# Direct transfers moved from GpSimd's queue to SyncE's and ScalarE's in a perceiver block with routed experts

## The chip, the cores and the metric

The kernel runs on one core of a Trainium2 chip. The metric is the time on the device in microseconds, of which the median of several runs is given. Three engines and the DMA queues matter here beside TensorE (PE): VectorE (DVE), ScalarE (ACT) and GpSimd (POOL) compute, and each of ScalarE, GpSimd and SyncE (SP) can also issue DMA transfers from its own queue of instructions, in the order in which they stand there.

## What is computed

All arrays are fp32. `x` has 8 batches of 64 rows of 512; `ctx_1024` has 8 batches of 1601 rows. The reference, cut to its three steps:

```python
x = x + xattn(layernorm(x), ctx_1024)   # 16 heads of 32; "stablemax" in place of softmax
x = x + attn(layernorm(x))              # 8 query heads of 64, one k and one v, causal softmax
x = x + ffn(layernorm(x))               # 2 shared experts (mean) + top 2 of 8 routed experts

# stablemax: s = where(x >= 0, x + 1, 1 / (1 - x));  s / sum(s)
# ffn:
shared = mean over 2 of gelu(xf @ sW1 + sb1) @ sW2 + sb2      # 512 -> 2048 -> 512
gates = xf @ rW + rb; the two largest, softmax of the two
moe = sum over the two of prob * (gelu(xf @ W1[e] + b1[e]) @ W2[e] + b2[e])
```

## The kernel before

The 512 rows of `x` stand in SBUF as `res`, four tiles of 128. The kernel has three stages.

**Attention.** The context is taken in 24 sections of 512 columns (three for each batch), each loaded as `cx` (L147) by SyncE. Keys and values of a section are made by `products` (L337): a product of two by two blocks in seven units, for which GpSimd makes differences of the context, `tx` (`context_part`, L313), and VectorE those of the weights. Scores of a section go through `convert` (L525): ScalarE splits them in sign, VectorE takes the reciprocal (L538), GpSimd adds (L539) and keeps the totals (L551). The first section is done plainly (`first_keys`, `first_values`), and between its units stand the norms of the four tiles (`first_rows`, L473: factors `ln_rs`, rows `xn`, transposed rows `xnT`) and the queries (`q_unit`, L484, the product `ps_q`). Each batch has 65 columns more than its three sections: 64 come in pairs of batches as `cxt` (`load_tail`, L421), and the last one of each batch, the odd column, is gathered at the start for all batches as `odd_x` (L415, four transfers of elements that lie apart in memory). Its value row is made once (`odd_v`) and copied by a transfer into the last row of the tail's values `vt` (L461). `clear` (L234), in the plan at the fourth batch, writes zeroes into the slots `xs` (4 MB in DRAM) and into one row each of `ys_d` and `yo_d`.

**Order.** A `Plan` holds the units of TensorE with a length each, and other steps with a due time; it calls them in that order. This is the order of the code's calls only: when the program is built, the framework places each instruction on its engine's queue by its own view of when it is ready, and allots buffers and waits. A queue is then run in that order, and an instruction that waits holds all behind it on its engine.

**Routing.** After the last norm the gates choose two experts for each row. VectorE works out a slot for each pair (`route`, L982), and GpSimd scatters the rows `xn` into `xs` with eight indirect transfers (L1069). The experts stand in the order of how many rows they have and get 256, 192, 160, 144 and four times 128 slots.

**Experts.** `run` (L1313) goes over the blocks: a shared expert on the last 128 rows (`Shared`), one half of the second shared expert (`Halves`), eight routed blocks (`Routed`), and the other half (`Halves`). A routed block takes 16 chunks of its hidden width; for each, TensorE makes `ps_h` (L1340), ScalarE takes the Gelu into `hT` (L1345), and TensorE adds the second product one chunk later (`second`). Weights come in quarters of 1 MB from SyncE (`w1t`, `w2t`, L775 and L783). Three steps move rows: `start` (L1259) fetches a block's rows `xg` from `xs` and transposes them, three chunks ahead of the block; `answer` (L1273) copies a result from PSUM to `yo` and writes it to `ys_d`; `turn` (L1304) first transposes results of blocks whose size is no multiple of 128, and is kept in the list `later` until chunk 3 of the block that follows. At the end `combine` (L1367) gathers the answers `g` from `ys_d` with eight indirect transfers and adds them to `res`, and `rows_out` stores it.

`xg`, `yo`, `g` and other tiles of 128 x 512 share five buffers (`sd`). All direct transfers of this account that are not named as SyncE's or ScalarE's are issued by GpSimd: biases and small weights at the start, `odd_x`, the zeroes, the rows into `vt`, `xg` and the answers. ScalarE issues only `wk`, `wv` and `wq` at the start.

Of the kernel before, what the change touches and what calls it, by code (L numbers as in the profile page):

```python
# [18 lines left out]
P = 128  # L19
# [9 lines left out]
NEXP, NSH = 8, 2  # L29
# [10 lines left out]
TAIL = SKV - NSEC * SEC  # L40
# [6 lines left out]
TOT = sum(CAPS)  # L47
# [28 lines left out]
def perceiver_kernel(  # L76
# [7 lines left out]
    nc = tc.nc  # L84
# [25 lines left out]
    def at4(name):  # L110
        return atp.tile([P, 1024], F32, tag="at", name=name)

    def np2(name):
        return npp.tile([P, 512], F32, tag="np", name=name)

    def sd(name):
        return sdp.tile([P, 512], F32, tag="sd", name=name)

    def psa(name):
        return ps_a.tile([P, 512], F32, tag="a", name=name)  # L120
# [35 lines left out]

    def bias_cols(src, n, name):
        t = const.tile([P, n], F32, name=name)
        nc.gpsimd.dma_start(out=t, in_=src)
        return t  # L160

    def bias_row(src, n, name):
        t = const.tile([P, n], F32, name=name)
        nc.gpsimd.dma_start(out=t, in_=src.partition_broadcast(P))
        return t

    bk_t = bias_cols(bk, NC, "bk_t")
    wv = load_w(wvT, "wv", nc.scalar)

    res = big.tile([P, NTT, E], F32, name="res")  # L170
    for tt in range(NTT):
        nc.sync.dma_start(out=res[:, tt, :], in_=x[tt * P : (tt + 1) * P, :])
    wq = load_w(wqT, "wq", nc.scalar)
    bq_t = bias_cols(bq, NC, "bq_t")
    bv_t = bias_cols(bv, NC, "bv_t")
    bo_t = sd("bo_t")
    nc.gpsimd.dma_start(out=bo_t, in_=bo.partition_broadcast(P))
    rb_t = bias_row(rb, NEXP, "rb_t")

    def load_small(src, name):  # L180
        t = const.tile([P, NC, src.shape[1]], F32, name=name)
        nc.gpsimd.dma_start(out=t, in_=src.rearrange("(c p) f -> p c f", p=P))
        return t

    rw_t = load_small(rW, "rw_t")
    b1_t = const.tile([P, NSH, NHC], F32, name="b1_t")
    nc.gpsimd.dma_start(out=b1_t, in_=sb1)

    ident = const.tile([P, P], F32, name="ident")
    make_identity(nc, ident)  # L190
# [11 lines left out]
    for j in range(2):  # L202
        m = mask[j * SQ : (j + 1) * SQ, 0, :]
        nc.gpsimd.affine_select(
            out=m, in_=m, compare_op=ALU.is_ge, fill=NEG, base=0,
# [10 lines left out]
        out=tri, in_=ones, compare_op=ALU.is_gt, fill=0.0, base=0,  # L216
# [12 lines left out]
    ys_d = dram.tile([TOT + 1, E], F32, name="ys_d")  # L229
    yo_d = dram.tile([P + 1, E], F32, name="yo_d")  # L230
# [3 lines left out]
    def clear():  # L234
        zero = np2("zero")
        nc.gpsimd.memset(zero, 0.0)
        nc.gpsimd.dma_start(
            out=xs.rearrange("(n p) e -> p n e", p=P),
            in_=zero.rearrange("p (o e) -> p o e", o=1).to_broadcast([P, ROWS // P, E]),
        )  # L240
        nc.gpsimd.dma_start(out=ys_d[TOT : TOT + 1, :], in_=zero[0:1, :])
        nc.gpsimd.dma_start(out=yo_d[P : P + 1, :], in_=zero[0:1, :])

    class Norm:

# [31 lines left out]
    def cols(t):  # L277
        return t.rearrange("p (c t) -> p c t", c=NC)
# [27 lines left out]
    def right_parts(x):  # L306
        return {"b11": x[:, 0:2, 0:HF], "b12": x[:, 0:2, HF:SEC],
                "b21": x[:, 2:4, 0:HF], "b22": x[:, 2:4, HF:SEC]}
# [101 lines left out]
    ROUND = TAIL - 1  # L410
# [1 line left out]

    odd_x = const.tile([P, NC, B], F32, name="odd_x")
    for c in range(NC):
        nc.gpsimd.dma_start(  # L415
            out=odd_x[:, c, :],
            in_=ctxT[:, c * P : (c + 1) * P, SKV - 1 : SKV].rearrange("b p s -> p (b s)"),
        )
    odd_v = const.tile([B, E], F32, name="odd_v")
# [31 lines left out]
    def tail_values(b):  # L451
        x = tails[b, "x"]
        ps = psa("ps_vt")
        for c in range(NC):
            nc.tensor.matmul(
                ps, x[:, c, 0 : 2 * ROUND], wv[:, c, :], start=c == 0, stop=c == NC - 1
            )
        for k in range(2):
            v = tails[b + k, "v"] = tlp.tile([P, E], F32, name="vt")
            nc.scalar.copy(v[:ROUND], ps[k * ROUND : (k + 1) * ROUND])  # L460
            nc.gpsimd.dma_start(out=v[ROUND:TAIL, :], in_=odd_v[b + k : b + k + 1, :])  # L461

    per = NSEC * SEC // P + 1

# [426 lines left out]
    for u, time in enumerate(when):  # L891
        plan.at(weighed[u], lambda u=u: weigh(*units[u]))
        plan.at(time, lambda u=u: begin(u))
        for j in range(1, 4):
            plan.at(time + 0.3 * j * wide[u] * step, lambda u=u, j=j: convert(*units[u], j))
        if u == 3 * nu:
            plan.at(time, clear)
    for tt in range(NTT):
        gap = 5.0 if tt < NTT - 1 else 3.2
        for bb in range(2):  # L900
            b = 2 * tt + bb
            last = (b + 1) * nu - 1
            done = weighed[last]
# [35 lines left out]
    from_i = gp.tile([P, 2, NTT], I32, name="from_i")  # L939
# [155 lines left out]
    class Shared:  # L1095
# [13 lines left out]
        def start(self):  # L1109
            self.x = xnT[:, :, self.tts[0] * P : self.tts[0] * P + self.n]  # L1110
# [21 lines left out]
    class Halves:  # L1132
# [55 lines left out]
        def combine(self):  # L1188

            k = len(self.right)  # L1190
            for q in self.qs:
                p = self.right[q] = right_parts(self.h[q])
                t = at4("ht").rearrange("p (k c s) -> p k c s", k=2, c=2)
                if not k:
                    self.t4 = at4("ht").rearrange("p (k c s) -> p k c s", k=2, c=2)
                p |= {"t1": t[:, 0], "t2": t[:, 1], "t3": p["b12"], "t4": self.t4[:, k]}
                k += 1
                for d, a, b in RIGHT:
                    nc.vector.tensor_tensor(p[d], p[a], p[b], ALU.subtract)
# [33 lines left out]
    class Routed:  # L1233
# [25 lines left out]
        def start(self):  # L1259
            self.x = at4("xgT").rearrange("p (c n) -> p c n", c=NC)  # L1260
            for s, w in self.parts:
                xg = sd("xg")
                nc.gpsimd.dma_start(out=xg[:w], in_=self.source(s, w))
                pt = cols(psx("pt_x"))
                for c in range(NC):
                    nc.tensor.transpose(pt[:, c, :w], xg[:w, c * P : (c + 1) * P], ident[:w, :w])  # L1266
                nc.vector.tensor_copy(self.x[:, :, s : s + w], pt[:, :, :w])  # L1267
            self.x = self.x[:, :, : self.n]
# [4 lines left out]
        def answer(self, s, w, src):  # L1273
            yo = sd("yo")
            nc.vector.tensor_copy(yo[:w], src)  # L1275
            nc.gpsimd.dma_start(out=self.dst[self.o0 + s : self.o0 + s + w, :], in_=yo[:w])  # L1276

        def second(self, hc, hT):
            first, last = hc == 0, hc == NHC - 1
# [28 lines left out]
                    nc.tensor.transpose(pt[:w, d, :], self.yT[:, d, s : s + w], ident)  # L1308
                self.answer(s, w, pt[:w].rearrange("p c d -> p (c d)"))

    later = []

    def run(blocks, at=None):  # L1313
        pending = None
        for n, blk in enumerate(blocks):
            if isinstance(blk, Halves):
                if n == 0:
                    blk.start()
                units = blk.units()
                for k, fn in enumerate(units):  # L1320
                    fn()
                    if pending is not None:
                        pending[0].second(*pending[1:])
                        pending = None
                    if at and (n, k) in at:
                        at[n, k]()
                    if k == 3:
                        while later:
                            later.pop(0)()
                    if k == len(units) - 3 and n + 1 < len(blocks):  # L1330
                        blocks[n + 1].start()
                continue
            for k, hc in enumerate(blk.hcs):
                w1t = blk.weights(hc // QC)[0]
                if k == 0 and n == 0:
                    blk.start()
                f = (hc % QC) * P
                ph = psa("ps_h")
                for c in range(NC):
                    nc.tensor.matmul(  # L1340
                        ph[:, : blk.n], w1t[:, c, f : f + P], blk.x[:, c, :],
                        start=c == 0, stop=c == NC - 1,
                    )
                hT = np2("hT")
                nc.scalar.activation(hT[:, : blk.n], ph[:, : blk.n], AF.Gelu, bias=blk.bias(hc))  # L1345
                if pending is not None:
                    pending[0].second(*pending[1:])
                pending = (blk, hc, hT)
                if at and (n, k) in at:
                    at[n, k]()  # L1350
                if k == 3:
                    while later:
                        later.pop(0)()
                if k == len(blk.hcs) - 3 and n + 1 < len(blocks):
                    blocks[n + 1].start()
        if pending is not None:
            pending[0].second(*pending[1:])
        while later:
            later.pop(0)()

    def expert_in(t, k):
        return lambda: nc.values_load(
# [19 lines left out]
    def routing():  # L1382
        for tt in range(NTT - 1):
# [10 lines left out]
            (0, 0): routing,  # L1394
            (2, 2): lambda: probabilities(tops.pop()),
            (2, 6): add_biases,
            (NEXP + 2, 1): lambda: combine(ys_d, from_i),
        },
    )

# [79 lines left out]
```

## Time and profile before

| | |
|---|---|
| time, median of 3 runs | 1409.54 us (1407.6 to 1409.95) |
| time of the profiled execution | 1412.35 us |
| its span | 1410.7 us |
| q1 (SyncE's queue) | 77732 packets, 136.94 MB |
| q0 (GpSimd's queue) | 4704 packets, 13.91 MB |
| q10 (ScalarE's queue) | 1632 packets, 3.15 MB |

Times of transfers, as the page gives them (median from issue to landing): `xs<-zero` 13.9 us, `xg<-xs` of 256 KB 6.9 us, `ys_d<-yo` of 256 KB 6.7 us, `odd_x` 7.9 us, `vt<-odd_v` 2.9 us, `w1t` of the routed experts 12.4 us, `wq` 15.0 us.

How to read the lines: times are microseconds unless a column is marked ns. A line of the timeline has start, length, engine, line of the code, operation, what it writes and reads, how many, and in brackets how long the engine was idle before it and what ended that. SPq and ACTq are the transfers that these engines issue; a transfer's length there is the time of its issue, not until it lands. A line of the waits has who waited for whom, the total, how many times and the longest. The chain is followed back from the last instruction, at each step to what released it; "issue" in it is time in which the engine waited for nothing that the profile shows. Numbers of buffers are left out of the names.

### The profile page before, as it was taken

How to read it: one execution, taken by the hardware profiler on the slowest of the kernel's cores; microseconds unless marked ns; L12 is line 12 of the kernel's file. 1: busy time of each engine (PE TensorE's matmuls, PEld its weight loads, DVE VectorE, ACT ScalarE, POOL GpSimd, SP SyncE). 2: the span in 40 equal slices, each digit the busy share in tenths (PEclk: the TensorE clock that was granted, in tenths of full speed). 3: DMA queues.
4: the chain of work that ended last, by engine and by line, in shares of the span. 5: the costliest groups of instructions: out<-in, count | busy, mean ns of one | idle time of the engine just before them, and what ended most of it. 6: DMA issues, size and time to landing. Idle time of an engine off the chain costs nothing.

```text
span 1410.7 us, 35571 instructions
## 1 busy us (share of the span) xinstructions
PE 1375.2 (97%) x15632; PEld 1084.2 (77%) x15632; DVE 887.1 (63%) x650; ACT 648.7 (46%) x1348; POOL 746.6 (53%) x672
## 2 busy tenths in 40 slices
PE   8999999999999999999999999999999999999996
PEld 3678788788788888788878877555786799977775
DVE  4698999898889997989988889514330000100331
ACT  3556566565666666765756567322211111122230
POOL 6388899885879886879886867400200000000020
PEclk9999999999999999999999999999999999999998
DMA  7002012102320121121121125353556256789620
GB/s 225 31 3 69 32 32 77 62 32 69 121 69 32 55 84 39 32 69 33 46 91 32 62 69 194 104 186 99 194 196 228 101 180 243 279 317 330 217 68 31
DMA packets 84226, 156.30 MB, mean 111 GB/s; under 512 B 13307, under 2 KB 13339, under 8 KB 84069
## 3 DMA queue, kind: packets, MB, share of 16 engines
q1 hardware_dynamic: 77732, 136.94, 28.5%
q0 software_dynamic: 4704, 13.91, 2.9%
q10 hardware_dynamic: 1632, 3.15, 0.7%
q8 instruction: 124, 2.03, 0.6%
q14 instruction: 34, 0.27, 0.1%
HBM read 143.24 MB, written 10.72 MB: 109 GB/s over the span
## 4 chain that ended last, share of the span: by engine, by line
PE 80%; issue 8%; DVE 4%; ACT 3%; POOL 3%; DMA 1%; POOLq 0%; DVEq 0%
PE ps_k L331 17%; PE ps_v L331 16%; PE ps_h L1340 8%; PE ps_s L520 5%; PE y L1294 4%; PE ps_hr L331 3%; PE ps_o L570 3%; PE ps_h L806 3%; PE y L1285 3%; PE y L818 3%; DVE neg L538 2%; PE ps_hh L331 2%; PE ps_v L399 1%; PE ps_k L389 1%; POOL tx L320 1%
## 5 line engine op out<-in xcount | busy, mean ns | idle before, releaser
L538 DVE RECIPROCAL neg<-neg 128x512 f32<-128x512 f32 (+1 forms) x224 | 684.0, 3092 | 65.5 <-ACT neg L537 57.4
L539 POOL TENSOR_TENSOR at<-at,neg 128x512 f32<-128x512 f32 (+1 forms) x224 | 266.6, 1195 | 136.8 <-DVE neg L538 129.4
L551 POOL TENSOR_TENSOR tot<-tot,at 128x512 f32<-128x512 f32 (+1 forms) x176 | 223.7, 1271 | 12.9
L1340 PEld LDWEIGHTS ps_h<-xgT,w1t 128*128 128x128 f32 x1024 | 147.8, 191 | 38.5 <-issue 33.2
L1345 ACT ACTIVATE hT<-ps_h,b1e 128x128 f32<-128x128 f32 (+4 forms) x128 | 50.3, 393 | 261.0 <-PE ps_h L1340 235.0
L537 ACT ACTIVATE neg<-neg,one_t 128x512 f32<-128x512 f32 (+1 forms) x224 | 161.3, 721 | 0.0
L1340 PE MATMUL ps_h<-xgT,w1t 128*128 128x128 f32 (+4 forms) x1024 | 160.7, 300 | 0.0
L535 ACT ACTIVATE neg<-ps_s 128x512 f32<-128x512 f32 (+1 forms) x224 | 129.5, 579 | 64.5 <-PE ps_s L520 53.8
L1276 POOL DMA_DIRECT2D ys_d<-yo x12 | 6.6, 546 | 287.2 <-DVE yo L1275 287.2
L331 PE MATMUL ps_k<-tx,sk 128*128 128x256 f32 x552 | 129.2, 385 | 5.7 <-ACT kT L348 5.7
L536 ACT ACTIVATE at<-ps_s 128x512 f32<-128x512 f32 (+1 forms) x224 | 130.9, 586 | 0.1
L331 PE MATMUL ps_v<-sv,tx 128*128 128x256 f32 x552 | 128.8, 384 | 0.0
L331 PEld LDWEIGHTS ps_k<-tx,sk 128*128 128x128 f32 x552 | 101.7, 190 | 24.8 <-ACT kT L348 3.8
L331 PEld LDWEIGHTS ps_v<-sv,tx 128*128 128x128 f32 x552 | 102.6, 190 | 16.5 <-issue 1.9
L1285 PE MATMUL y<-w2t,hT 128*128 128x512 f32 x192 | 96.5, 597 | 0.0
L1267 DVE COPY xgT<-pt_x 128x512 f32<-128x512 f32 (+3 forms) x12 | 6.8, 593 | 142.7 <-PE pt_x L1266 142.7
L348 ACT ACTIVATE kT<-ps_k,bk_t 128x256 f32<-128x256 f32 x138 | 59.4, 496 | 69.1 <-PE ps_k L331 69.1
L344 ACT COPY v<-ps_v 128x512 f32<-128x512 f32 x92 | 55.6, 604 | 70.2 <-PE ps_v L331 70.2
L331 PE MATMUL ps_k<-cx,wk 128*128 128x256 f32 x368 | 86.7, 385 | 0.0
L331 PE MATMUL ps_v<-wv,cx 128*128 128x256 f32 x368 | 86.3, 383 | 0.0
L520 PEld LDWEIGHTS ps_s<-qT,kT 32*64 32x64 f32 x6144 | 70.0, 130 | 19.2 <-issue 17.6
L520 PE MATMUL ps_s<-qT,kT 32*64 32x64 f32 x6144 | 76.9, 231 | 2.4 <-issue 1.6
(263 smaller groups left out, 2035.7 us busy)
## 6 DMA issues: line engine op xcount, KB each, us to landing
w1t<-in_W_dram SPq DMA_DIRECT2D x32, 1024.0 KB, 12.4
w2t<-in_W_dram SPq DMA_DIRECT2D x32, 1024.0 KB, 12.3
cx<-in_ctxT_dram SPq DMA_DIRECT2D x23, 1024.0 KB, 5.7
w1t<-in_sW_dram SPq DMA_DIRECT2D x12, 1024.0 KB, 5.4
w2t<-in_sW_dram SPq DMA_DIRECT2D x12, 1024.0 KB, 5.6
wo<-in_woT_dram SPq DMA_DIRECT2D x4, 1024.0 KB, 5.5
awq<-in_aWq_dram SPq DMA_DIRECT2D x4, 1024.0 KB, 5.5
awp<-in_aWp_dram SPq DMA_DIRECT2D x4, 1024.0 KB, 5.4
```

The costliest lines, as they stand in the source:

```text
L331: nc.tensor.matmul(ps[:, k, :], l[:, c, k * P : (k + 1) * P], r[:, c, :], start=first and k == 0 and c == 0, stop=last and c == 1, skip_gr ...
L348: nc.scalar.activation(dst[:, k], src[:, k], AF.Identity, bias=bk_t[:, g : g + 1])
L520: nc.tensor.matmul(ps[j][h, k, g, :], kT[rows, g, h], qT[rows, g, b * SQ : (b + 1) * SQ], start=True, stop=True, skip_group_check=True,)
L535: nc.scalar.activation(neg, ps, AF.Relu, scale=-1.0)
L536: nc.scalar.activation(pos, ps, AF.Relu)
L537: nc.scalar.activation(neg, neg, AF.Identity, bias=one_t[:w])
L538: nc.vector.reciprocal(neg, neg)
L539: nc.gpsimd.tensor_add(pos, pos, neg)
L551: nc.gpsimd.tensor_add(tot, tot, at[:, :, i])
L1285: nc.tensor.matmul(self.y[k], hT[:, s : s + w], w2t, start=first, stop=last)
L1294: nc.tensor.matmul(y[d // 2][:, d % 2, :], w2t[:, d * P : (d + 1) * P], hT[:, : self.n], start=first and d % 2 == 0, stop=last, skip_group ...
L1340: nc.tensor.matmul(ph[:, : blk.n], w1t[:, c, f : f + P], blk.x[:, c, :], start=c == 0, stop=c == NC - 1,)
```

## The change

Every direct transfer leaves GpSimd's queue; the sixteen indirect ones stay. Biases, small weights, the zeroes and the rows into `vt` go to SyncE, `odd_x`, `xg` and the answers to ScalarE. An answer's transfer is no longer asked for by `answer` itself: it is put in a list `done`, which is emptied at chunk 6 of a routed block, or at unit 2 of a `Halves` block, where `later` is now emptied too (before: unit 3). The last `combine` is called two units later.

```diff
 def bias_cols(src, n, name):
-        nc.gpsimd.dma_start(out=t, in_=src)
+        nc.sync.dma_start(out=t, in_=src)
...
 def bias_row(src, n, name):
-        nc.gpsimd.dma_start(out=t, in_=src.partition_broadcast(P))
+        nc.sync.dma_start(out=t, in_=src.partition_broadcast(P))
...
-    nc.gpsimd.dma_start(out=bo_t, in_=bo.partition_broadcast(P))
+    nc.sync.dma_start(out=bo_t, in_=bo.partition_broadcast(P))
...
 def load_small(src, name):
-        nc.gpsimd.dma_start(out=t, in_=src.rearrange("(c p) f -> p c f", p=P))
+        nc.sync.dma_start(out=t, in_=src.rearrange("(c p) f -> p c f", p=P))
...
-    nc.gpsimd.dma_start(out=b1_t, in_=sb1)
+    nc.sync.dma_start(out=b1_t, in_=sb1)
...
 def clear():
         nc.gpsimd.memset(zero, 0.0)
-        nc.gpsimd.dma_start(
+        nc.sync.dma_start(
             out=xs.rearrange("(n p) e -> p n e", p=P),
...
-        nc.gpsimd.dma_start(out=ys_d[TOT : TOT + 1, :], in_=zero[0:1, :])
-        nc.gpsimd.dma_start(out=yo_d[P : P + 1, :], in_=zero[0:1, :])
+        nc.sync.dma_start(out=ys_d[TOT : TOT + 1, :], in_=zero[0:1, :])
+        nc.sync.dma_start(out=yo_d[P : P + 1, :], in_=zero[0:1, :])
...
     for c in range(NC):
-        nc.gpsimd.dma_start(
+        nc.scalar.dma_start(
             out=odd_x[:, c, :],
...
-            nc.gpsimd.dma_start(out=v[ROUND:TAIL, :], in_=odd_v[b + k : b + k + 1, :])
+            nc.sync.dma_start(out=v[ROUND:TAIL, :], in_=odd_v[b + k : b + k + 1, :])
...
                 xg = sd("xg")
-                nc.gpsimd.dma_start(out=xg[:w], in_=self.source(s, w))
+                nc.scalar.dma_start(out=xg[:w], in_=self.source(s, w))
...
         def answer(self, s, w, src):
             yo = sd("yo")
             nc.vector.tensor_copy(yo[:w], src)
-            nc.gpsimd.dma_start(out=self.dst[self.o0 + s : self.o0 + s + w, :], in_=yo[:w])
+            done.append(
+                lambda: nc.scalar.dma_start(
+                    out=self.dst[self.o0 + s : self.o0 + s + w, :], in_=yo[:w]
+                )
+            )
...
-    later = []
+    later, done = [], []
+
+    def flush(todo):
+        while todo:
+            todo.pop(0)()
...
-                    if k == 3:
-                        while later:
-                            later.pop(0)()
+                    if k == 2:
+                        flush(later)
+                        flush(done)
...
                 if k == 3:
-                    while later:
-                        later.pop(0)()
+                    flush(later)
+                if k == 6:
+                    flush(done)
...
-            (NEXP + 2, 1): lambda: combine(ys_d, from_i),
+            (NEXP + 2, 3): lambda: combine(ys_d, from_i),
```

More of the change, by code (lines that the diff above doesn't have):

```diff
@@ L1357, in run @@
             pending[0].second(*pending[1:])
-        while later:
-            later.pop(0)()
+        flush(later)
+        flush(done)
     def expert_in(t, k):
```

## The prediction

> **What bounds the kernel now.** I read the page first, then the chain, then the busy table by stage, then timelines and waits where a moved transfer lies.
>
> ```profile
> span 1410.7 us, 35571 instructions
> PE 1375.2 (97%) x15632; PEld 1084.2 (77%) x15632; DVE 887.1 (63%) x650; ACT 648.7 (46%) x1348; POOL 746.6 (53%) x672
> PE 80%; issue 8%; DVE 4%; ACT 3%; POOL 3%; DMA 1%; POOLq 0%; DVEq 0%
> ```
>
> TensorE is the bound; GpSimd (POOL) holds 3% of the chain. By stage: from 120 to 860 us (attention) PE is busy 97 to 99%, VectorE about 90%, POOL about 81%; from 1100 to 1340 us (experts) PE 240.0 of 240, ScalarE (ACT) 44 and POOL 10. So POOL's issues can matter only in attention; a ScalarE that stands still can matter everywhere, as PE waits for its copies and Gelus.
>
> Two facts decide the rest. First, a transfer on a hardware queue (SyncE's or ScalarE's) waits for an unrelated earlier one. Waits of SyncE's queue up to 60 us (total us, times, longest):
>
> ```profile
> SPq L147 <- DMA wv<-in_wvT_dram: 4.4, 1, 4.4
> SPq L172 <- DMA cx<-in_ctxT_dram: 4.3, 3, 2.5
> SPq L425 <- DMA cx<-in_ctxT_dram: 3.1, 1, 3.1
> SPq L147 <- DMA res<-in_x_dram: 0.4, 1, 0.4
> ```
>
> No buffer explains them (res is not cx). Counting both hardware queues together, the issues alternate cx, wk (eight in all), res, wv, res, wq, res, res, cxt, cxt, cx, cx. Each that waits does so for the one eight places before: the ninth (res) for the first cx, the fifteenth (cxt) for the last of the first cx, the seventeenth (cx) for the first res, the eighteenth for wv. ScalarE's timeline (start, length) shows the same from inside:
>
> ```profile
> 0.92 1.86 ACTq L134 DMA_DIRECT2D wk<-in_wkT_dram  x4
> 5.41 0.39 ACTq L134 DMA_DIRECT2D wv<-in_wvT_dram  x1
> 8.44 0.39 ACTq L134 DMA_DIRECT2D wq<-in_wqT_dram  x1
> 8.85 1.28 ACT L258 ACT_TABLE_LOAD   x1 [8.85 <-DMA wk<-in_wkT_dram]
> 14.08 0.29 ACT L258 ACTIVATE ln_rs<-ln_mv,eps_t 128x1 f32<-128x1 f32 x1 [3.95 <-DVE ln_mv L254]
> ```
>
> wq stood until a wk chunk had landed, and the table load stood behind it.
>
> Second, a queue's order is not the code's: the framework places an instruction where it believes it ready. The four ln_rs precede the kT copies that stand ahead of them in the code; the first vt rows go out at 86 us, their ps_vt product runs at 120. That belief is early for transfers: near the end the first two adds of gathered rows are placed before the join of a unit whose matmuls end at 1354.2 us, and the second waits for its row until 1356.4. The place that this endangers:
>
> ```profile
> 989.00 1.10 POOL L1069 DMA_INDIRECT xs<-xn,slot_i  x1 [71.72 <-DVE from_i L1054]
> ...
> 1019.82 0.97 POOL L1069 DMA_INDIRECT xs<-xn,slot_i  x1 [2.01 <-DMA xs<-xn,slot_i]
> 1027.28 1.72 POOL L1263 DMA_DIRECT2D xg<-xs  x3 [6.49 <-PE ps_hh L331]
> ```
>
> xg reads the slots, so it waits for the eighth scatter; the matmul named as releaser touches neither, so I take the scatter's landing, 1027.3 us. POOL could stand there for nothing. ScalarE has this at that time:
>
> ```profile
> 1013.23 0.59 ACT L1180 COPY hq<-ps_hh 128x512 f32<-128x512 f32 x1
> 1014.96 0.59 ACT L1180 COPY hq<-ps_hh 128x512 f32<-128x512 f32 x1 [1.14 <-PE ps_hh L331]
> 1017.48 0.91 ACT L1158 ACTIVATE hq<-hq,b_t 128x256 f32<-128x256 f32 x2 [1.94 <-DVE hq L1164]
> ...
> 1059.05 0.47 ACT L1345 ACTIVATE hT<-ps_h,b1e 128x256 f32<-128x256 f32 x1 [25.99 <-issue]
> ```
>
> **Part 1: what leaves POOL.** In the first 12 us: seven bias issues of 0.57 to 0.82 us and four of odd_x at 0.89. POOL then idles 10.5 us before its first add, so removing them is worth 0. In attention: eight vt at 0.54 (4.3) and the zeroes at 1.22 + 0.51 + 0.49 (2.2), together 6.5 us of a POOL that is 81% busy. Only the zeroes are seen on the chain:
>
> ```profile
> 365.28 1.74 issue
> 367.56 5.01 DVE neg L538 x2
> ```
>
> The big zero runs from 365.78 to 367.01, and the add behind it frees the buffer that the reciprocal waits for. Between 0 and -6.5 I take -1.8, that piece. In the experts, 24 issues at 0.55 leave a POOL that is idle: 0.
>
> **Part 2: SyncE takes biases, zeroes, odd rows.** After the start its queue is free around each: no issue between 331 and 396 us, where the 4 MB of zeroes (13.9 us to landing) go out; the vt of 161, 378, 547, 589 and 759 us lie at or between its loads, and wait for the same buffer that ScalarE's copy of vt waits for today. A context load held by 3 us is used some 20 us later. So 0; without that cover, up to 3 each. The Trainium skill (DMA: Bandwidth & Descriptors, Latency and other measured facts) puts the first byte at about 0.6 us on the hardware path against about 1 us on the software path. By that rule each moved transfer saves 0.4 us, at most 0.4 us for the one answer that the chain waits for at the end. The rows say more than first bytes decides: the last answer takes 2.3 us to land on POOL's queue, a median answer 6.7 beside the weight loads. I count 0.
>
> **Part 3: the start on ScalarE.** odd_x adds four issues behind wq, the biases seven on SyncE. With the alternation kept, the order after the first eight is bk, wv, res, wq, res, odd, res, odd, res, odd, bq, odd. By the rule of eight the third odd waits for wv (landed at 17.9, when the last cx was let go) and the fourth for wq, 8.44 + 15.0 = 23.4 us. Behind it on ScalarE stand the table load (1.28), the ln_rs pair, and everything up to the xnT copies, which PE's q needs. Free at 23.9, table load to 25.1, two ln_rs and VectorE's answer to 26.4; from the first xn to the last xnT copy took 20.87 to 29.87, 9.0 us: 35.4 instead of 29.9. So +5.5. If one transfer falls elsewhere and the fourth odd gets another predecessor, ScalarE is free by 18 and the loss is 0; a cost below 0 is excluded only for this wait, and odd_x's small pieces, landing after wq, could add 2 to 3. Ends 0 and +8. The second context load slips from 13 to about 30 us, lands by 36, and its differences (6.9 us on POOL) are done by 43; PE wants them at 56.
>
> **Part 4: routed rows on ScalarE.** Undisturbed scatters follow each other every 3.0 to 3.8 us; three of the eight took 6 to 7 beside the weight loads. An order that believes in the undisturbed pace has the last landed at 989 + 7 x 3.1 + 3.4 = 1014. xg then stands between the copies of the unit at 1013 to 1015 and ScalarE stops there until 1027.3: 13.3 us. Behind it are this unit's copies and Gelus; PE's next product adds into the bank that the copy reads, so PE has about 2 us of its own: +11. PE then runs without a gap to 1344, so nothing returns it. Ends: 0, if the place falls into ScalarE's 26 us without work before 1059; +17, if it falls at 1008. I take 11, the undisturbed row. Here a rule and a row part. The skill's rule (same page, Issuing engines are not separate DMA queues) is that the issuing engine only saves issue time; by it, moving xg costs 12 issues of 0.4 us, hidden in ScalarE's 1.38 us gaps, and the sum of this part is 0. But the page also says (Anatomy of one DMA) that the wait for a semaphore is the issuing sequencer's; the 6.49 us that POOL stood before xg is such a wait, and by it the sum is 11. I follow the row.
>
> **Part 5: experts and end.** Twelve xg and twelve answers are 24 x 0.4 = 9.6 us of ScalarE beside 1.38 us of idleness before every Gelu: hidden, unless an issue meets a transfer eight places back in flight (weights take 12.4 us to land) or is slow as SyncE's are behind full queues (up to 3.6). Ends 0 and 8 blocks x (3.4 - 1.4) = 16; I take +1.5, one such wait. At the end the answer is asked for after unit 2 rather than at once, combine after unit 3; as these are placed where ready and units 2 and 3 need nothing of VectorE, I count 0, ends -0.5 and +3 (the issue after unit 2's copy at 1351.4 instead of 1348.3).
>
> Sum: -1.8 + 5.5 + 11 + 1.5 = +16.2. The profiled execution took 1412.35 us around its span of 1410.7; it would take 1428.6. It lies 2.8 above the median of 1409.54, so the forecast for the median is 1425.7, rounded 1426.
>
> **The rivals.** (A) as summed, 0.45. (B) Only the start: xg falls into ScalarE's free 26 us, or the framework counts the weight loads' share and places it late: -1.8 + 5.5 + 0.5, about 1414. For it: PE's row products leave ScalarE idle just after 1033; against: the two adds placed too early. 0.27. (C) Faster: POOL is the hidden bound of attention, and the 6.5 us taken off it come off the path, at -1.8 to -6.5; it decides if neither odd_x nor xg meets a pending transfer on ScalarE. For it: POOL's tx stands on the chain in several pieces of 2.5 to 3.7 us; against: POOL has only 3% of the chain. About 1404, 0.18. (D) ScalarE's issues stick in every block: A + 16, 1442, 0.10. That the change does not do what it says is small: the 16 indirect transfers stay on POOL, and nothing else without indices does.
>
> **How the numbers follow.** About 0.2% (2.8 us) is what a measurement here can tell from no change. A and D, and most of B, are slower: 0.72. B's low end (start lost only in part) and C's high end are the same: 0.12. The rest of C: 0.16. The range 1405 to 1437 leaves out D and the lower half of C; A alone would span 1418 to 1437.
>
> **What would show it.** Start: ScalarE's table load after 20 us and ps_q after 35. Routing: ScalarE idle for some 10 us before xg or the copy behind it, with PE idle beside it, between 1008 and 1040. Attention: the 1.74 us piece at 365 gone. I am wrong if ScalarE's first ln_rs stays near 14 us and xg falls behind the last hq Gelu; then B's smaller part or C holds.

## The result and the profile after

The changed kernel takes 1430.02 us (median of 5 runs, 1425.54 to 1431.27) against 1409.54. The ratio on record is 1.0128, with a 95% interval of 1.0115 to 1.0141; it is not formed from these two medians, whose quotient is 1.0145. By either the kernel is slower. The profiled execution took 1430.02 us around a span of 1428.3, 17.6 more than the 1410.7 of before. The page after begins so, and these are its rows of queues and of the chain:

```profile
span 1428.3 us, 35569 instructions
PE 1381.6 (97%) x15632; PEld 1087.4 (76%) x15632; DVE 880.6 (62%) x650; ACT 647.5 (45%) x1348; POOL 716.7 (50%) x626
...
q10 hardware_dynamic: 8704, 8.34, 1.8%
q0 software_dynamic: 1280, 4.20, 0.9%
...
PE 82%; DVE 5%; DMA 3%; ACT 3%; POOL 3%; issue 3%; ACTq 0%; POOLq 0%; DVEq 0%
```

The transfers have moved as intended: GpSimd (POOL) is busy for 30 us less and its software queue q0 keeps the 16 indirect transfers alone. TensorE (PE) is busy for 6.4 us more with the same 15632 matmuls, and DMA has risen from 1% to 3% of the chain.

Between milestones that both traces have, the 17.6 us are these:

| stretch | before | after | difference |
|---|---|---|---|
| span's start to the first `ps_q` | 30.46 | 36.58 | +6.1 |
| to the first `ps_kt` | 84.96 | 86.02 | +1.1 |
| attention, to the third round's `ps_ap` | 704.71 | 704.61 | -0.1 |
| to the next shared expert's first `ps_h` | 44.40 | 46.08 | +1.7 |
| to the last shared Gelu | 141.86 | 140.96 | -0.9 |
| to the first routed Gelu | 52.66 | 63.10 | +10.4 |
| routed experts, to the last half's `ps_hh` | 285.50 | 285.50 | 0.0 |
| to its `ps_hr` | 30.10 | 33.79 | +3.7 |
| to VectorE's last add | 24.37 | 24.37 | 0.0 |
| to the end of the span | 11.68 | 7.29 | -4.4 |

**The start.** ScalarE's timeline after (start, length, and in brackets the idle time before it and its releaser):

```profile
0.80 0.49 ACTq L415 DMA_DIRECT2D odd_x<-in_ctxT_dram  x1
1.32 3.13 ACTq L134 DMA_DIRECT2D wk<-in_wkT_dram  x4
...
16.46 2.28 ACTq L415 DMA_DIRECT2D odd_x<-in_ctxT_dram  x3
18.77 1.28 ACT L258 ACT_TABLE_LOAD   x1 [18.77 <-DMA odd_x<-in_ctxT_dram]
20.79 1.52 ACT L266 ACTIVATE xn<-res,ln_nb,ln_rs 128x512 f32<-128x512 f32 x2 [0.24 <-DVE ln_nb L261]
...
27.44 0.81 ACT L266 ACTIVATE xn<-res,ln_nb,ln_rs 128x512 f32<-128x512 f32 x1 [2.47 <-DVE ln_nb L261]
```

The same rows before:

```profile
20.87 1.52 ACT L266 ACTIVATE xn<-res,ln_nb,ln_rs 128x512 f32<-128x512 f32 x2 [3.86 <-DVE ln_nb L261]
23.10 0.81 ACT L266 ACTIVATE xn<-res,ln_nb,ln_rs 128x512 f32<-128x512 f32 x1 [0.33 <-DVE ln_nb L261]
```

ScalarE stood before the odd rows until 16.46, and its table load began at 18.77 instead of 8.85. Yet the first xn came at 20.79, as before (20.87). The third came 4.3 us later than the 23.10 of before: it waited for VectorE's `ln_nb`. VectorE's timeline shows what that stood behind:

```profile
21.15 1.27 DVE L303 TENSOR_TENSOR sk<-wk 128x512 f32<-128x512 f32 x2
...
25.36 0.68 DVE L303 TENSOR_TENSOR sv<-wv,sv 128x512 f32<-128x512 f32 x1
25.96 0.21 DVE L259 RECIPROCAL ln_rs<-ln_rs 128x1 f32<-128x1 f32 x2
```

Before, the reciprocals of the second pair ran at 22.61 and 22.98, ahead of these weight differences:

```profile
22.61 0.16 DVE L259 RECIPROCAL ln_rs<-ln_rs 128x1 f32<-128x1 f32 x1 [1.29 <-ACT ln_rs L258]
...
24.21 2.37 DVE L303 TENSOR_TENSOR sk<-wk 128x512 f32<-128x512 f32 x2
```

Now the framework has written them behind, as if it believed ScalarE's answer to be late. TensorE waits meanwhile, as its timeline shows:

```profile
25.58 1.04 PE L274 MATMUL pt<-ident,xn 128*128 128x128 f32 x8
28.31 0.66 PE L274 MATMUL pt<-ident,xn 128*128 128x128 f32 x4 [1.69 <-ACT xn L266]
30.96 0.66 PE L274 MATMUL pt<-ident,xn 128*128 128x128 f32 x4 [1.99 <-ACT xn L266]
31.45 5.30 PE L399 MATMUL ps_v<-wv,cx 128*128 128x512 f32 x8
```

From 8.85 us to the first `ps_q`, PE idles 3.68 us, where it had none, and is busy for 2.44 us more. Of the latter, 1.6 us is in the last `ps_v` group, 5.30 where before shows 3.70: the clock was at half for 3.4 us from 31.6.

```profile
26.92 3.70 PE L399 MATMUL ps_v<-wv,cx 128*128 128x512 f32 x8
```

**The routing.** ScalarE after:

```profile
1016.78 0.58 ACT L1180 COPY hq<-ps_hh 128x512 f32<-128x512 f32 x1 [2.16 <-PE ps_hh L331]
1028.54 0.83 ACTq L1263 DMA_DIRECT2D xg<-xs  x2
1029.43 0.91 ACT L1158 ACTIVATE hq<-hq,b_t 128x256 f32<-128x256 f32 x2 [12.06 <-DMA xs<-xn,slot_i]
1030.24 1.05 ACT L1180 COPY hq<-ps_hh 128x512 f32<-128x512 f32 x2
```

ScalarE does no work for 12.06 us: it stands before the two row loads until the last scatter has landed (1028.52), and issues them, with a Gelu and two copies behind. PE over the same stretch, in three parts (busy time of PE is the second number after the range; the granted clock is the third from the end):

```profile
1014.25:1024.90 10.65, 8.53 (x36) 6.46 (x34) 1.38 (x2) 0.95 (x2) 1.92 (x2) 1.00 0.77 271
1024.90:1035.10 10.20, 4.24 (x10) 3.45 (x11) 0.00 (x1) 1.86 (x4) 0.96 (x1) 0.50 0.25 78
1035.10:1077.35 42.25, 42.25 (x201) 37.24 (x201) 14.66 (x22) 7.97 (x18) 0.00 (x0) 1.00 0.51 167
sum 63.10, PE 55.03 PEld 47.15 DVE 16.04 ACT 10.78 POOL 2.87; mean PE 18.34 PEld 15.72 DVE 5.35 ACT 3.59 POOL 0.96
```

The same 246 matmuls took 52.66 us before, without a gap:

```profile
1006.39:1059.05 52.66, 52.66 (x246) 45.70 (x245) 16.04 (x24) 11.00 (x24) 5.64 (x8) 1.00 0.64 212
```

So the 10.4 us are 8.07 of standing still (63.10 - 55.03) and 2.37 of slower work (55.03 - 52.66), as the clock fell to 0.50 during the pause and stayed there until 1035.1, for the first 4.24 us of the work that followed.

### The profile page after: what moved, and what is told of

It is laid out like the page before. It is cut to its first block, busy times and chain, and to the rows that moved or that the text cites. A ratio compares the mean times of both kernels' runs of the same rounds, so it can differ in the third digit from the quotient of the medians.

```text
span 1428.3 us, 35569 instructions
## 1 busy us (share of the span) xinstructions
PE 1381.6 (97%) x15632; PEld 1087.4 (76%) x15632; DVE 880.6 (62%) x650; ACT 647.5 (45%) x1348; POOL 716.7 (50%) x626
## 4 chain that ended last, share of the span: by engine, by line
PE 82%; DVE 5%; DMA 3%; ACT 3%; POOL 3%; issue 3%; ACTq 0%; POOLq 0%; DVEq 0%
PE ps_k L331 18%; PE ps_v L331 16%; PE ps_h L1349 10%; PE y L1289 6%; PE ps_s L520 5%; PE y L1298 4%; PE ps_hr L331 3%; PE ps_o L570 3%; PE ps_h L806 3%; PE y L818 3%; DVE neg L538 2%; PE ps_hh L331 2%; DMA xs<-xn,slot_i 2%; PE ps_v L399 1%; POOL tx L320 1%
## 5 line engine op out<-in xcount | busy, mean ns | idle before, releaser
L551 POOL TENSOR_TENSOR tot<-tot,at 128x512 f32<-128x512 f32 (+1 forms) x176 | 223.4, 1269 | 12.9
L1382 POOL DMA_INDIRECT g<-ys_d,from_i x8 | 8.7, 1092 | 344.8 <-PE ps_hh L331 342.6
## 6 DMA issues: line engine op xcount, KB each, us to landing
w1t<-in_W_dram SPq DMA_DIRECT2D x32, 1024.0 KB, 11.5
```

Of the source, the lines that this page charges most:

```text
L551: nc.gpsimd.tensor_add(tot, tot, at[:, :, i])
```

## The experiments

The theory: the whole loss comes from two moves, the odd rows and the routed rows on ScalarE, each of which makes an engine with work of its own stand before a transfer. The rivals: the loss needs the other moves too (biases and zeroes on SyncE, answers on ScalarE), or the two losses overlap. The twelve runs, each timed beside the kernel before (whose medians there are 1410.23, 1410.50 and 1410.38; the ratios are not formed from the medians):

| kernel | median us | ratio to before | 95% interval |
|---|---|---|---|
| odd_pool | 1419.44 | 1.0067 | 1.0054 to 1.0080 |
| late_parts | 1422.29 | 1.0086 | 1.0073 to 1.0099 |
| first_xg_pool | 1417.11 | 1.0052 | 1.0039 to 1.0065 |
| xg_late | 1414.31 | 1.0036 | 1.0022 to 1.0050 |
| only_xg_act | 1422.71 | 1.0090 | 1.0077 to 1.0103 |
| only_odd_act | 1419.72 | 1.0063 | 1.0050 to 1.0076 |
| only_attn_sp | 1411.05 | 1.0000 | 0.9991 to 1.0008 |
| only_bias_sp | 1409.25 | 0.9992 | 0.9982 to 1.0002 |
| only_answers_act | 1410.48 | 0.9997 | 0.9986 to 1.0008 |
| odd_pool_xg_late | 1408.50 | 0.9981 | 0.9969 to 0.9993 |
| odd_sp_xg_late | 1409.78 | 0.9989 | 0.9979 to 0.9999 |
| best_40 | 1415.67 | 1.0036 | 1.0023 to 1.0049 |

### Undoing parts of the change

**odd_pool**, the changed kernel with the odd rows back:

```
     for c in range(NC):
-        nc.scalar.dma_start(
+        nc.gpsimd.dma_start(
             out=odd_x[:, c, :],
```

> The changed kernel with odd_x alone back on GpSimd's queue. My theory: odd_x on ScalarE is the whole loss at the start (queries begin at 36.6 us instead of 30.5), so the queries begin at about 30.5 us again and the time falls from 1430 by 6 to about 1424. Rival, the seven bias transfers ahead of and between the rows of x on SyncE: the start stays late and the time stays at 1430.

`ps_q` starts at 29.56, with PE busy for all of the 20.71 us before it at full clock; the order on VectorE and ScalarE is that of before. The routing loss stays (62.92 us from the last shared to the first routed Gelu). So the 6.1 us to the first `ps_q` are the odd rows' alone; of the 1.1 us after it 0.7 stay here. The time fell by 10.6 us, more than the 6 of the forecast. This profile also lacks the half-clock stretch at 1387 us (below); no run shows that the odd rows caused it.

**late_parts**, the changed kernel with the weight differences asked for later in the plan, so that VectorE's order is again that of before:

```
-    plan.at(0.05, lambda: (wkp.update(weight_parts(wk, "sk")), wvp.update(weight_parts(wv, "sv"))))
+    plan.at(5 * FULL + 2.05, lambda: (wkp.update(weight_parts(wk, "sk")), wvp.update(weight_parts(wv, "sv"))))
```

> The changed kernel with odd_x still on ScalarE, but the differences of the first weights (sk, sv) called after the norms of the four tiles. The prediction's reading, ScalarE held behind odd_x until about 18.8 us and all that follows: nothing changes, 1430. The other reading, the order on VectorE, where the norm factors of the last two tiles stand behind eight weight differences (21.2 to 26.0 us): these factors come about 4 us earlier, the queries begin near 33.5 us and the time falls by about 3 to 1427.

ScalarE still stands until 18.94, but `ps_q` starts at 32.13. VectorE's timeline here:

```profile
23.83 0.16 DVE L259 RECIPROCAL ln_rs<-ln_rs 128x1 f32<-128x1 f32 x1 [2.43 <-ACT ln_rs L258]
...
25.87 0.16 DVE L259 RECIPROCAL ln_rs<-ln_rs 128x1 f32<-128x1 f32 x1 [1.68 <-ACT ln_rs L258]
```

The second pair no longer stands behind the differences, and the clock stays full. So of the 6.1 us at the start, 4.4 (36.58 - 32.13) come from the order on VectorE that the move brought about and the pauses that followed. The other 1.7 (32.13 - 30.46) are left with the wait, and with ScalarE's own order, in which `kT` copies still stand ahead of the second pair's factors; no run parts these two. The time fell by 7.7 us, more than the 4.4: the profile, of the fastest of its five executions, has no half-clock stretch at 844, 1103 or 1387 us either, and in it the three rows of the table with these stretches are 1.7, 1.7 and 4.0 us shorter than in the changed kernel.

**first_xg_pool**, the changed kernel with the first block's two row loads on GpSimd, the other ten on ScalarE:

```
-                nc.scalar.dma_start(out=xg[:w], in_=self.source(s, w))
+                (nc.gpsimd if isinstance(self.r0, int) and self.r0 == 0 else nc.scalar).dma_start(
+                    out=xg[:w], in_=self.source(s, w)
+                )
```

> The changed kernel with the two xg transfers of the first routed block on GpSimd, the other ten still on ScalarE. My theory, ScalarE stands 12 us before these two because they wait for the last scatter: the loss between the last Gelu of the shared block and the first routed Gelu (63.1 us against 52.7) goes, the time falls by 10.4 to about 1420. Rival, every xg on ScalarE costs about 1 us, or the expert weights come late: it stays above 1427.

The stretch to the first routed Gelu is 52.66 us again, to the hundredth that of before: two transfers of twelve make the whole loss there.

**xg_late** keeps all twelve on ScalarE, but holds the first block's two behind the last Gelu of the half-block, by a copy of one element into the buffer that they overwrite:

```
+                if isinstance(self.r0, int) and self.r0 == 0:
+                    nc.scalar.copy(xg[0:1, 0:1], self.behind[0:1, 3, 0:1])
                 nc.scalar.dma_start(out=xg[:w], in_=self.source(s, w))
...
+                        blocks[n + 1].behind = blk.h[blk.qs[-1]]
```

> The changed kernel with all xg on ScalarE, but the first block's two held behind the last Gelu of the half block before it, by a copy of one element of its result into each xg tile ahead of the transfer (it is overwritten). ScalarE has 26 us without work there. If the place in ScalarE's order is the cause and not the engine: as first_xg_pool, 1420. If any wait for a scatter on ScalarE costs, or the later fetch makes the transposes late (they have stood at about 1067 us): 1425 or more.

The loads go out at 1038.99, in ScalarE's free time, and PE's row for the stretch is whole again:

```profile
1012.07:1064.68 52.61, 52.61 (x245) 45.67 (x244) 16.06 (x24) 11.29 (x26) 2.89 (x3) 1.00 0.60 206
```

So ScalarE's queue is no worse for these loads than GpSimd's; their place on it was. The times fell by 12.9 us in first_xg_pool and 15.7 here, more than the 10.4 of the stretch: both profiles also lack the half-clock stretches at 844 and 1387 us, which no run ties to these loads.

### One part alone on the kernel before

**only_xg_act** and **only_odd_act** move only the line of `xg`, or only that of `odd_x`, to ScalarE:

```
-                nc.gpsimd.dma_start(out=xg[:w], in_=self.source(s, w))
+                nc.scalar.dma_start(out=xg[:w], in_=self.source(s, w))
```

> The kernel before with the routed rows' twelve loads alone moved to ScalarE's queue. Theory: the whole routing loss of 10.4 us comes with this one line, less 12 x 0.082 = 1.0 us of GpSimd's last DRAIN: about 1419, ScalarE standing some 12 us at the first load and the stretch from the last shared Gelu to the first routed one 63 us instead of 52.7. Rival (the loss needs the other moved transfers, the answers on ScalarE or the late start): 1409 to 1411.

> The kernel before with the four odd rows of the start alone moved to ScalarE's queue. Theory: the start's loss comes with this one line, q at about 36.6 instead of 30.5 and about 1 us more to the first kt, less 4 x 0.082 = 0.3 us of DRAIN: about 1416. Rival (the biases that move to SyncE's queue make the start late, the odd rows only stand behind wq): 1409 to 1411, q at 31 or earlier.

ScalarE's timeline in only_xg_act has the wait of the changed kernel:

```profile
1020.82 0.83 ACTq L1263 DMA_DIRECT2D xg<-xs  x2
1021.70 0.91 ACT L1158 ACTIVATE hq<-hq,b_t 128x256 f32<-128x256 f32 x2 [13.62 <-DMA xs<-xn,slot_i]
```

The stretch takes 65.42 us, 12.8 more than before, and the time rises by some 12.7 (0.90% of 1410.5). Neither the answers nor the late start are needed. The loss is somewhat larger than forecast, as this scatter landed later against ScalarE's work (13.62 us of standing, 12.06 in the changed kernel).

In only_odd_act `ps_q` starts at 40.91, 10.4 us late, not 6. ScalarE there:

```profile
13.13 8.89 ACTq L415 DMA_DIRECT2D odd_x<-in_ctxT_dram  x3
22.05 1.28 ACT L258 ACT_TABLE_LOAD   x1 [22.05 <-DMA odd_x<-in_ctxT_dram]
```

From the first of these three issues to the end of the last there are 8.89 us, in the changed kernel 2.28, so ScalarE was free at 22. Of these, 4.7 us pass between the first issue and the second, which by its semaphore waits for `wv`, and the last issue alone takes 3.41. VectorE's order was that of the changed kernel (the second pair's reciprocals at 29.26, behind the differences). The time rose by 8.9 us (0.63%), while this one profile's span is only 5.4 longer: the routed experts took 283.81 us in it, 1.7 less than in before, with no stretch at half clock there, the shared experts 0.9 less, attention 0.9 less, and the end 1.1 less. The rival is refuted: the biases need not move for the start to be late.

**only_attn_sp** moves the zeroes and the odd rows of v to SyncE, **only_bias_sp** the seven biases (each is that `nc.gpsimd` becomes `nc.sync` in the lines of the change), and **only_answers_act** takes the change's `answer`, `done`, `flush` and the later `combine`, and nothing else.

> The kernel before with the three zeroes and the eight odd rows of v alone moved to SyncE's queue. Theory now: GpSimd's piece of 1.74 us on the chain at 365 us gives nothing, since the stretch from the first kt to the third ap was as long in both kernels (704.7 and 704.6); only the last DRAIN shortens, by 11 x 0.082 = 0.9 us: 1408.6 to 1409. The prediction's step (the piece goes whole, 1.8 us) and the DRAIN together: 1406.8, with that stretch at 703. A third possibility, transfers that SyncE holds up behind waits for v: slower than 1411.

> The kernel before with the seven bias loads alone moved to SyncE's queue. Theory: nothing is lost, since no engine stands behind SyncE's waits; the order on PE, VectorE and ScalarE stays, q starts at 29.5 to 30.5, the last DRAIN is shorter by 7 x 0.082 = 0.6 us: about 1409.5. Rival (the biases push the input rows and context loads on SyncE back by the wait for the transfer eight places before): q at 32 or later, 1412.

> The kernel before with the routed answers' twelve stores alone moved to ScalarE's queue, at the places that the change gives them, and the combine moved with them. Theory: hidden, and GpSimd's last DRAIN shorter by 12 x 0.082 = 1.0 us, 5.14 to 4.15: about 1409.5. Rival (a store sticks behind a transfer eight places back and ScalarE's Gelu waits, or the later combine shows at the end): 1413 or more.

None can be told from no change. In only_attn_sp the stretch from the first `ps_kt` to the third round's `ps_ap` takes 704.06 us, against 704.71 and 704.61: the 1.8 us of the prediction's first step do not appear. In only_bias_sp `ps_q` starts at 30.43. In only_answers_act the end is 1.6 us shorter, but the last half-block takes 33.42 us to its `ps_hr` (30.10 before), and the two cancel.

### Both mends, and the end of the kernel

**odd_pool_xg_late** joins the edits of odd_pool and xg_late; **odd_sp_xg_late** has the odd rows on SyncE's queue instead.

> The changed kernel with both mends: the four odd rows of the start are back on GpSimd's queue, and the first block's two row loads, still on ScalarE's, are held behind the last half-block Gelu by a one-element copy. Everything else of the change stays. Theory (two separate losses, the order of the start and ScalarE standing still at the row loads, and one gain, GpSimd's last DRAIN, which in six profiles lasts about 60 ns plus 82 ns for each transfer that GpSimd issued: 62 in the kernel before, 5.136 us; 16 in the changed one, 1.376 us): the span of the run with the row loads held, 1411.9, less the 7.1 us by which q starts earlier with the odd rows on GpSimd (29.6 for 36.7), plus 0.3 us of DRAIN for four transfers: 1405.1, and 1.5 to 2 us more as time: about 1407, faster than the kernel before by 0.2 to 0.4%. Rival (the two losses overlap: an earlier start only makes a later wait longer): 1411 or more.

> The mended kernel with the four odd rows on SyncE's queue instead of GpSimd's; the order of work on the other engines stays the same. Theory (what costs is that an engine with work of its own, ScalarE, stands behind the odd rows, not that they sit in a hardware queue): q at 29.3 to 30.5 as with GpSimd, 1408.2, of which 0.3 us is the shorter DRAIN. Rival (the odd rows in a hardware queue push the context loads behind them back, and those are late for the second round): q up to 30.5 but 2 to 5 us lost before the first kt, 1411 to 1413.

The first is 0.19% faster than the kernel before, about what a measurement here can tell from none: its span is 1405.9, `ps_q` starts at 29.35, and the stretch of the routing takes 52.60. The losses do not overlap. In the second, SyncE's timeline shows that the odd rows go out late there too:

```profile
15.13 0.36 SPq L187 DMA_DIRECT2D b_t<-in_sb_dram  x1
16.58 3.03 SPq L415 DMA_DIRECT2D odd_x<-in_ctxT_dram  x4
```

They go out from 16.58 to 19.61, behind SyncE's other waits and as late as ScalarE's three did (16.46), and `ps_q` still starts at 29.49. Its ratio, 0.9989, cannot be told from the 0.9981 of the first. The late issue costs nothing on an engine that has no work of its own. This tells the two readings of the start apart: not the hardware queue is what costs, but who stands in front of it.

**The 4.4 us at the end.** In the kernel before, the last rows of the output have landed 4.8 us after the start of VectorE's last add, but the span ends 11.7 us after it. The trace has GpSimd's last long instruction in between, a DRAIN that the page doesn't list: it begins after that landing, and in all fourteen profiles the span ends 0.8 us after it. Against the number of transfers that GpSimd issues in the whole kernel, in thirteen kernels:

```
transfers issued by GpSimd    last DRAIN, us
16  (after, late_parts, xg_late, odd_sp_xg_late)    1.376
18  (first_xg_pool)                                 1.542
20  (odd_pool, odd_pool_xg_late)                    1.706
50  (only_xg_act, only_answers_act)                 4.156
51  (only_attn_sp)                                  4.237
55  (only_bias_sp)                                  4.564
58  (only_odd_act)                                  4.809
62  (before)                                        5.136
```

That is 82 ns for each transfer, (5.136 - 1.376) / 46, and at no transfers the same line leaves 0.07 us. **best_40** tests it by adding 40 transfers of 512 bytes to odd_pool_xg_late, asked for in the experts, where GpSimd idles:

```
+                if k in (8, 10, 12, 14) and 2 <= n <= 6:
+                    for _ in range(2):
+                        nc.gpsimd.dma_start(out=extra.pop(), in_=ident[0:1, :])
```

> The mended kernel (odd rows back on GpSimd's queue, first row loads held) with 40 transfers more, of 512 bytes each, issued by GpSimd while it idles in the routed experts; nobody reads what they write. Theory (GpSimd's last DRAIN costs 82 ns for each transfer that GpSimd has issued in the whole kernel, and the end of the kernel waits for it): DRAIN of 1.71 + 40 x 0.082 = 4.98 us instead of 1.71, the time from VectorE's last instruction to the end 11.5 us instead of 8.2, and the time 1408.5 + 3.3 = 1411.8, nothing else changed. Rival 1 (the DRAIN follows the bytes or packets of the software queue, or the transfers still in flight near the end): 1408.5, DRAIN near 1.7. Rival 2 (the extra transfers disturb the weight loads): the routed experts take over 286 us.

They did not go out there. As they need nothing, the framework placed all 40 between 6.6 and 46.8 us, as GpSimd's transfers in the profile show:

```profile
6.61 2.00 POOL L1371 DMA_DIRECT2D extra_d<-ident  x4
...
38.68 8.61 POOL L1371 DMA_DIRECT2D extra_d<-ident  x18
```

That makes the test harder for the theory, and it holds: with 60 transfers the DRAIN lasts 4.972 us (4.98 expected), and the end takes 10.92 us instead of 8.21 (11.5 expected; the DRAIN began 0.5 us sooner after VectorE's last add). Bytes, packets and transfers in flight are ruled out: 40 of 512 bytes, issued over 1350 us earlier, cost as much each as those of 256 KB. The time rose by 7.2 us, 3.9 more than the DRAIN. The profile puts 2.1 into the start (`ps_q` at 31.41), where the extra transfers stand among GpSimd's first adds, and 3.2 into the last half-block, with 6.8 us at half clock there. That the extra transfers made the start late is likely, but no run takes it apart.

## Why the prediction was right, and where it was not

The prediction's +16.2 us stands against +17.6 in the profiles, and 1426 against 1430.02. Step by step:

- **Part 1, the zeroes off GpSimd's path (-1.8): failed; 0.** I read the "issue" row of 1.74 us on the chain at 365 us as GpSimd's transfer. The chain after, where that transfer is on SyncE, has the same row:

```profile
370.58 1.53 DVE neg L538
372.11 1.74 issue
373.85 0.31 DVE v L377
```

  VectorE's timeline of before shows what it was:

```profile
363.75 3.35 DVE L538 RECIPROCAL neg<-neg 128x512 f32<-128x512 f32 x1 [2.35 <-POOL at L539]
367.02 0.63 DVE L377 TENSOR_TENSOR v<-ps_v,v 128x512 f32<-128x512 f32 x1
```

  One reciprocal of 3.35 us, which the chain shows as 1.53 of work and 1.74 of "issue". The transfer lay beside it. Asking that engine's own timeline would have shown it before.
- **Part 2, SyncE takes the small transfers at no cost: right.** only_attn_sp and only_bias_sp bear it out (1.0000 and 0.9992).
- **Part 3, the start (+5.5): the size near (+6.1, and 1.1 more to the first `ps_kt`), the mechanism half wrong.** ScalarE's wait for a transfer in front was there, but ended 5 us earlier than I had it (table load at 18.77, not 23.9). One odd row went out ahead of `wk`, and by the semaphores in the trace the last one waited for `bo_t` (landed at 18.35), not for `wq`. As the first norm pair of before waits for the rows of `x` until 20.9 anyway, the wait alone would have cost some 1.7 (late_parts against before). What I left out is that moving four instructions let the framework write VectorE's and ScalarE's work in another order, and what pauses do to the clock. That 5.5 came near 6.1 is luck.
- **Part 4, the routing (+11): the mechanism right, +10.4, but two of its terms missed and cancelled.** ScalarE stopped between a copy and a Gelu until the eighth scatter had landed, as said. But the place was one step earlier than I had it, behind the copy that before has at 1008.92, for which I had named +17:

```profile
1008.92 0.59 ACT L1180 COPY hq<-ps_hh 128x512 f32<-128x512 f32 x1 [2.16 <-PE ps_hh L331]
```

  And the eighth scatter, which I took from before, landed at 1028.52 instead of 1026.67, 1.9 us later, while the work around it came 7.9 later. From the end of that copy to the landing this makes 11.2 us, where the trace of before, with the same copy and its own scatter, would have made 17.2. Why it landed sooner no run shows. PE stood for 8.07 us, not 11, and the clock took 2.37 more. The Trainium skill's rule (DMA: Bandwidth & Descriptors, Issuing engines are not separate DMA queues) that another issuing engine only saves issue time would have given 0; only_xg_act measures 0.90%.
- **Part 5, the experts (+1.5): failed; 0.0** (285.50 us in both). Ten row loads and twelve answers hide in ScalarE's gaps completely.
- **The end: the -4.4 us were not foreseen at all.** GpSimd's DRAIN explains 3.76 (5.136 - 1.376); the rest is that it began 0.66 us sooner after the last add (5.10 for 5.76). The +3.7 in the last half-block, for which I had allowed up to 3 with the later combine, is seen in four of the nine profiles with that combine and in none of the five without it (33.0 to 33.8 us, else 28.9 to 30.2), each time with 6.8 us at half clock. That the later combine makes this more likely is argued, not shown.

That the misses cancel is luck: 1.8 for Part 1, 1.7 at the start, 0.8 in the shared experts and 3.7 in the last half-block against 0.6 for Part 4, 1.5 for Part 5 and 4.4 at the end. That A was the case, of the four, is not: its two terms are the two moves that cost, each shown alone.

## What to carry over

A transfer takes its wait along when it moves to another engine's queue, so ask what work stands behind it there. The row loads cost 10.4 us where ScalarE's copies and Gelus stood behind them, and nothing behind its last Gelu; the odd rows made the start late on ScalarE, and not on SyncE. Where a framework orders instructions by when it believes them ready, look at the built order of every engine after a move, not only at the queue that was changed. Before a chain's "issue" row is credited to a neighbour, check in that engine's own timeline whether it was simply still busy.

## What the runs showed of the hardware

- **GpSimd's last DRAIN** takes 82 ns for each transfer that GpSimd has issued since the start, from 1.376 us for 16 to 5.136 for 62, whatever their size and however long ago, and the kernel's end waits for it.
- **The granted clock falls in steps.** Up to VectorE's last instructions, the records of the granted clock show only full and half, and every stretch at half lasts 3.4 us or a multiple of it:

```
before            976.1 for 6.8   1085.3 for 3.4   1358.4 for 3.4
after             31.6 for 3.4   844.0 for 3.4   987.3 for 3.4   1024.9 for 10.2
                  1103.4 for 3.4   1386.7 for 6.8
odd_pool_xg_late  834.5 for 3.4   977.9 for 3.4   1083.7 for 3.4
```

  The Trainium skill (TensorE: Matmul & The Clock Gate, What's actually happening) gives a window of 3413 ns that runs freely, and the trace agrees: in each profile the stretches begin whole multiples of 3.413 us apart (31.6 and 844.0 after, 238 of them). So the same short gap can cost 1.7 us in one kernel and nothing in another: from the third `ps_ap` on, the changed kernel has a stretch at 844 us, PE is busy for 43.77 us instead of 42.08 with the same work, and the kernel before, whose PE idles as long there (2.32 us, after 2.31), has none. When the windows are counted on from each profile's stretches, the one in which this gap begins has PE busy for 1.45 us in the kernel before, where the gap lies across the window's end, and for 1.10 in the changed one, where it lies within the window:

```profile
832.74:836.15 3.41, 1.45 (x7) 0.94 (x5) 3.41 (x3) 3.41 (x8) 1.27 (x1) 1.00 0.50 191
840.59:844.00 3.41, 1.10 (x6) 0.67 (x5) 3.41 (x3) 3.41 (x8) 1.27 (x1) 1.00 0.26 102
```

  In the fourteen profiles half clock follows this gap in the five where PE is busy for 1.37 us or less in one window, and in none of the nine where it is busy for 1.44 or more in each.
- **Half clock also follows matmuls of few rows.** At 1085 us before (1103 after) PE stands nowhere, but multiplies with 10 rows instead of 128:

```profile
1080.85 3.70 PE L1087 MATMUL ps_b<-b_t,wT 10*128 10x512 f32 x8
```

  In the eleven profiles where 2.5 us or more of this lie in one window a stretch at half follows; in late_parts, only_xg_act and only_odd_act, where the window's end parts it more evenly (2.1 us at most), none does, and the routed experts take 283.8 us instead of 285.5.
- **The noise of one profile.** Single profiles of this kernel can therefore differ by some 2 to 4 us, by where the windows fall.
